# Adding the products of four pairs of states ahead of W_out, with other ranks and tiles, in a four-layer kernel

## The chip, the cores and the metric

The kernel runs on one core of a Trainium2 chip. Time is device time of one execution in microseconds. TensorE is called PE here (its weight loads PEld), VectorE DVE, ScalarE ACT, GpSimd POOL, and SyncE, which issues most DMAs, SP.

## The reference

The input is 16 sequences of 256 tokens of width 128, all float32. Four residual layers follow each other, each on a layer norm of x:

- attention whose softmax weights are summed to one over the keys and multiplied with the query's own v, so that it amounts to a linear map: `x + norm(x) @ W_v @ W_out + b`;
- a mixture of 8 experts with hidden width 512, of which each token takes its best two by gate logits, weighted by a softmax over the two: `sum_e w_e * relu(x @ w1[e]) @ w2[e]`;
- a selective state space with 16 states: `delta = softplus(...)`, for each state n a scan over the 256 positions of a sequence, and

```
xs = cumsum(dB_u * dA_cumsum, axis=1) / (dA_cumsum + 1e-12)
y = einsum('bldn,bln->bld', xs, C) + u * D
out = y @ W_out + b_out
```

- a second mixture of experts with the same weights and the same kind of gate.

## The kernel before

The 4096 tokens are cut into eight blocks of 512 (two sequences). In the first experts' layer the blocks are taken in the groups `FIRST = ([0], [1], [2, 3], [4, 5], [6, 7])`, in the second in `SECOND = ([0, 1], [2, 3], [4, 5], [6], [7])`. `attention` and `gate` prepare blocks, `route` ranks the tokens of each expert and scatters their rows to a DRAM buffer `slots` (POOL's indirect DMAs), `experts` works through a group's eight experts, `collect` gathers two rows for each token (POOL again) and adds them to x, `mixer` is the state space of one block, and `finish` stores a block.

`SLOTS` gives the room for each expert in a group of one, two, three or four blocks, for each of the two layers. A room over 512 or 128 rows is divided evenly: 192 becomes two tiles of 96 rows, 330 three of 110, 216 two of 108, 384 three of 128. In `experts` an SP DMA fetches a tile `xs` from `slots`; PE transposes it; four matmuls with w1 (`ps_b<-xsT,w_s`), relu `h`, four matmuls with w2 that add up in one bank (`ps_y<-h,w_s`), a copy `yT`, transposes back, a copy `yr`, and an SP DMA to `ys`, from which `collect` gathers (`yy<-ys`). A group's gathers wait for its last `ys`. If an expert has more tokens than its room, a general path runs behind the kernel.

In `mixer` the 16 states are worked off in eight pairs. For a pair, ACT makes two decays and two `th` (tanh); PE spreads the rows of B and C over the partitions (`ps_B`, `ps_C`, two bf16 matmuls each); DVE multiplies `ps_B` by `du`, scans it with the decay into `w`, makes `ps_C = (th + 1) * ps_C` and `th = ps_C * w`. `th` has four buffers, `w` three, the decay two, `ps_B` and `ps_C` one each. Ahead of the pairs a block makes `delta`, `z`, `lt` and `du`, and one matmul with W_out's scaled copy `wsd_s` starts `ps_s`.

The products `th` of two pairs are added up (`ADD = 2`), and then two matmuls with `wsh_s` add the two halves to `ps_s`:

```
group.append(th)
if len(group) > 1:
    product(group[0], group[0], th, ALU.add)
if len(group) == ADD:
    for k in range(2):
        matmul(so, wsh_s, group[0][:, k, :], False, n + k == NS - 1)
    group = []
```

Nothing is issued where it is written. Each operation is recorded as a job of a class `Plan`, with the engines that may do it. `product` may go to POOL or DVE, `copy` and `relu` to ACT or DVE, and normalizing to ACT or DVE. `ORDER` is a long string of packed ranks, one for each job; `Plan.order()` places the jobs in time by these ranks, with a duration for each from `cost()` (DVE, ACT, POOL) and from `matmul`, and so settles both the order on each engine and which engine does a job. The program is then issued in that order. So the ranks and the durations matter to the program only through this order and these choices. For that reason all jobs have the same line in the profile, L710, but for the scatters (L807), the gathers (L821) and a few others. The functions that the change touches and their callers:

Of the kernel before, what the change touches and what calls it, by code (L numbers as in the profile page):

```python
# [10 lines left out]
F32 = mybir.dt.float32  # L11
# [3 lines left out]
AF = mybir.ActivationFunctionType  # L15
ALU = mybir.AluOpType
# [12 lines left out]
SECOND = ([0, 1], [2, 3], [4, 5], [6], [7])  # L29


SLOTS = ((192, 330, 480, 632), (216, 384, 600, 800))
UNIT = 2
ADD = 2
JOIN = 2
ACC = 0
POOLED = (3,)
# [3 lines left out]
XN, ROW, XS, XT, H, YT, DEPTH = 4, 3, 4, 3, 4, 3, 3  # L41

ORDER = (
    "c-oy;3zS?{m92a3_kHWtzxw}AcS6!hI-~;z$O;57;6V8Q2_u0S5d^_uSc)<WMU9}iM3yW-9GO9x!6gH;R9KFnMgszpL;?f?f"
    "k*<R^Xq@t@4Y*x(n)u9Rdv$gbywAU_uY5jJ?HGR&pu3!7%XbbZAPKv1@3dL7-PWr9y>~ce89&%(C@K%Jo9!(hVu?i`7ck&TU"
    "=}!eF%Vl)_8eOGlzoV+GCP40*uyj))&`!j{^V`L0}L96gZ<4gs;O)2b>A*3(6>rA1qHftKE)g1PD&+d4C53zj>tYtuRmST4)"
    "&WZ=i;-Wdt8&k}Jkz4frZfW0dx>2F9<qDP7bBq>YMzaZlQu8;l;?+ePSH#x<oKoEc04YdQ9_z#2UcR8YkQZ@_JKUIwrXpCBw"
    "y%n$|z+H*Fet87`^C*_nH1fcC_oYqiEa5-i%s&Llw`v@46X#t7>ItB=v6B`tD>z8D<E*H}0f-#>loAIJY14hsV+|<5QxV>F6"
    ">MACb|KehA*xQaiirRK`r;~{cLjneDt0Nf|kEoo*U@p9_j!i#dWsezvrR+sxshv)zuWsGhFh-7pml~U+|6RMg#e{BnBi1OJ8"
    "{AtKz1A~GTIhQXQRn%ke_1+;3-()<bWZJRR6xkpvtH^UoJyCT1TFBd-vKZw{l=N5^8I7n;k;oMd;@Ct0ds)?$Q&UmPXz}F6#"  # L50
    "dW9?-*SWOvxor10@uUMTT|4)h($^?t#9+p%<8@UwC4u_H&;{uTgXsAMiMbl@4dSA0RXZ4ACKM^vhG!qIZ3nF^_^|>`d-Tn&K"
    "wyzk<LlLQRB1Sh~zY_bopU;AF}%AS(s#+{Wm8iwK;{49U2`nGz1AY|+UEUrmJ%G;LyF9NZ`WH88wyQ>luGWVmKT3OV<!#{EW"
    "z!NIr5>A!W@A}UR$AWI|yFk+BEncN=R!(&QNPwlz&?wY>(L5$Xj@WkfMZ5@g#l8cWfdX#yell3CZhJqETdv4Sl?uKS~-)v})"
    "*4Vd22ckBKk|8VVy=0BLVS=}uE1S@ZYfgCSgm>u8<lgqPqc<;kc?rNJurWMKMhvbR2qEm+|2UcJKs<96Vvpuj0d3D4Ol{~jD"
    "cbd9cbIWM858=Cz7YhCRBII%{;(YO>*0hKYgrutqLc+%P%RBi3%*?jzD0>I3<3Efd@<bwI+I<3KauaD-H2gE37^e)@TEs7Rl"
    "mCTe(M@e{Hq2=o>!CxJnq#en9mpN*lS+&Iw2j!+`ts4{f2PVMHH#yYYq^BZsi=|-|t8(JfC6;{iqKJpA{YQK>8{db}Y7%1%m"
    "$WPD1#pR5Rju3=MF*JyEdPx|=W?&I655)808;G9f7ezWWA3XfwvOg@aHMUvd&5l5TnkS>p^$u;L$4aYP5jbo}#ADG_H0DKuj"
    "u!Z7tjkurLfov96nM^nzTX@8{Q$937vRW0C-5uOb^Oj3%l#B4<#!j~c5E#e_fwC;J+RCpwK|NPft1JPleU~<FVRNIdf6eaz_"
    "Nv0P>Z+A!CEICH}&6*u~1??PyUf7eg8@uY%b;<r%k|>f-k1T$sZg1Me)YxXVdWNeW?%8tuHdp{3#ogBbYA;w0bivzZvubm=S"
    ";u|tWYNdXxF6B#=HHK)3%~O5?RK;+SsOX+qgTI%sagY#bZ33c{lh?fXeo(UeK9XlQ!l>}&R7jB33OpT{afUf*+^D_6L!6*c<"  # L60
    "h7L9m@!!-^s_fy|QfmDvDt?3h}Vp{*$OLDcCS%nsc8svmPfsu)&;TDFcKF;EU}a@<8*34~xXDg|A}%sHpKTeo9dE`>kiXNE!"
    "2}Rao~0CdHr>Vh5vv;!0oyH0!d8k45OvgXmyL7+J<Yl^FG(U|O>XL3Z^p+mWlK0Gj2vl>bFE98-Xh<|d<ttXm_ycw_46$d*="
    "N{H*TW<G$1MvHzy|X*oCAKl|_DUET4E2{EZ~6~SV(+hdkJ2eiw&E}+CZo)u}D7<-j8X)h}#*5`2TRY(d%ak`I(om3YX7XQ;-"
    "82r-(aOFxjFT(DFH3&d<{WUmyg<*(gK;*T8E51PH6`c5O%$++arQY0k=N}_YL3^ZMXC|Hk8Tkp7kug{EMoc)KVA>SNEd*jOR"
    "9YC!pixRCZz|TuC8>TjE2Sd2j>|k}_jex`*77FX%xVN5;iP64HL+aT94Q(>1jRGe9_6W#Uzmtbw}b7x^s&|tS_9HVKCt5A<r"
    ";K3#2~{Q$LJJ~Hs`_xjttq@*ZSwWyjf2SC@AZj@tRoMK)SD!2#kI>vgzGf`??{<_J?ayD>|GN-@g6sACYC`O>cGby6Yag{&{"
    "i}+$XP#SP|(-qF~Kw%fXLgv}ls@Vcf(y{7%z2MX{bU?!9o?c~7re&u%04nm5av&iTz*iXBTg#+qYc$6S5>Z_diGZg@Lf6Z@l"
    ")wW4G;Y_;oS5sUq}{^J@BankP?#tvB!n0-i|(&S41wf@8QeqzI@v|6^xKn>E_@SbQwN(5yWll87$l4ZQ+dV~^R$DnXlPzYRo"
    ")nh#23O4sr7AdIyNKVav-OU8V&iXsz8B^JL-v%twpAwQ=Qp|pL-T}0+fY4v3M`J_Ct2}NOAeM^U#$*H;)v^arT5v56Py~LZy"
    "KtG#Z#A8=wV{w6{Aq2UK4;F$;&&I4XD{lhb2fGEE&R*a#-{EVssn+QktixhOrgXABzgXo6auRe$x$=KXq4BsUH~Xp{8b1kln"  # L70
    "N+6lChLhmik8mt@M}Y;tMZR#K=n$X_u5IpFss8+P{mW+v!LiI0f_TD5d!MEHHWJ{fMhI2>AeM8WT~lFC&MDJMTtfyM<#FVQG"
    "6lvYlzEg5Xy?ijwILJC0%|7jEaAdM4HQ9Ul^>ZtxO2d*7_vQ`_~SaB^+CfzpN?51RLemBMwz*BO@dmSRRDbMiV)Q)90R8v)z"
    "PHZ9pW?~U#))Iqb7HGfO(OYbK0V2jtFoI3HtT9vb*jfliR`xD_|=fpUst#pJqUfuD|?7`1i9dy4PmcQ6C_ua2TI`NL#X@*mg"
    "FRefEuh)`e$Qz<7@yzC)%_k#wz7<VN(?nT?jN!h38#$$@B&A}fNhKD)_V3C>6?W_Km;UG4d2i226s4(^Prc~oj9DzqGETcK8"
    "l1I%Z`po^mmqr`!`l4Z+3U}RBpKnhl}a~$D~2#N!gR!o$meVKHLX;2^h2XY87cFhMkAv)*fxxquK9mk7i_+QICRJ`ksSbxqM"
    "*I8qi^KK9B8|S>`kad*b*wWhc}`O7B-;)d)e~yQKVGI!z@(HG(2T0$>Pb^WShXEOR;`2lv#Y9kQb>_Ogj2i=fq_yU67CeVZr"
    "{@gsGEVbJj_oU$d>DPTCh!;?-g}h~-P|d6M0v5E0K_4$xYQ1gxnot`W$KR~PH@`L`l|7UC;<sTQxWUQ6||poTy22!i!IhKzy"
    "pXQf3l-Gg!A-@Dv~rsY^rO)gVE@UZZmD)VdP0}msHuac5QY{JGYJL#qvpHEjmiedOSa1F&HY|ulVc)O@cHts`I{@eiBjwR(!"
    "_8ix^k!l0(h~&T7vM4e5KVN*DYOK3E+dhbWdb3?O^7)&A1eAW?=7Vz!2K8hi*_g1DL}BPd81oY)3j%rzwa6$#het4-Ihzya7"
    "77H$j6raj9Caxc6jsy)rla2BZ#kLR!ussM?-TivyE_K=-%6eQ%Dy}IKPmF8KGQE(BPY{&sD0aUkypJowK$5&pz3Zxld!;r4b"  # L80
    "i{@8#QJ_IFn*;{VzcdLVpURg@j=$V-dy;p8g9$&<0E*5r}RnW4ssP!0vkwhv!q5M?mqtJQ-&7z$ANdJr>3`CNU5J!(3K065A"
    "i+L-$}&JeEnTAef=kA}-sw&-e>J#HChX&52<yMomPBiDcydpfxkF<esn+mybj<nYg@AEfou;>8oatI$$gl&*zUTVA&_w=>d0"
    ")VuxalN-e>{1?hHd#T<gEY603Sq;ya#Gqh_Mm3NVtcv12paWEAp@N;jl_QKli;?LCjg<s`!{TB$IU6ISyA=LpWVI7x57}ZFu"
    "UyR@ii5A&vj>Y+kR=nMcOp1blceu7K&ZmLJKbnmXE#R8F_*sih9<z#X+;A%6{A{Ez$^$XzqzsgPamGSd;v$zQUxv|TBU}pJO"
    "amc?{~0On8j*%t>`(S5uz_(gF0ig2eO`~@C)l`YfsL7i$mXvUPy{QQMzyN>t{N*$*BV(<B)RH{Zi?qJ-47zZD6A6QTNl6PX5"
    "ISpC}NRp5Pnd{WL_F(JZ&*EA26kJwh%tbQBz`jL{MqK*a1OmW2Y&=;)dCIpY+M<9hn6WW0SGk%=for-_rsND|HXUrYeDY^Wt"
    "uRc9iXm1sqF%8mqwdiz%BgB3yFq0D1xK{)d$SD=|z!!`R#$kn*RmVr&^uNvVT^94rO$#9JszL!=M5ANyV03eex*#vqAJ5%Ny"
    "4jqAju=(&N=4uCL$VU#40LZNbPG?#1NILG;DwkqZqSz2uCi;rN@$1`Lu><|JJbQm8p-oY1<G0KV!2gME%*-8+W+2sVI7iO}V"
    "by#4#`*ZG+D5_>`9E(B_QH4OGPsRbTmB)28Dj{m%J|AhKbS}aVhfpCwQ3T%8MPLEt0_hZ!m=-&iwY`GPJ764^K~`KA)|>;ZT"
    "@}ro$BSFRTs>(OgIUG3@gF-FYys&tR|0K7L5=Q1R;Acpqk2X^1mlt)<4r;#9V#Ar;xBaY8bA8LwH`k|bnD=W9={Cqp~?6mho"  # L90
    "&4_Wy<Nnt3%6`4o`d?Jc7`~W)6IU(A0xWeYE66moHm&C{%Swf1)8>zM4L0V)e(guDC4q`lQj5u0A+aaZ8un3Qd1Ymv1sxdPR"
    "bXpF`2ny4=hvZmZ(jB1TFvQ!y*3d@871G&uZwjyQCLcvtak_0a06QK|H{u2@M=iF$eXLNf~A_>t8mIX5}CBwCXxTAHI}2I<h"
    "`E~}xkx}PS^I0)w{z$;7M(mMgE@bH1*P=z1LhC|cMJ}fL|GOVkadMHZ|Iwe#A`toNgp%6N%#M5OoJ7Xx|oBi^Al<r1{j)cBY"
    "l~?L1sL<2Fxe}N<G+K_!DGWB1<tAJ`9fwY^rJe?ox=L6Hjs_FgT9+F+bp=uascEUaWHugt_1Qsn0t`Y``6H-EgwhO|E(3LFi"
    "Z?4fSLUZ9QdC9!r$s_l{2aE7_!YHqVmIU{%F`z!%!=I%kKZ5%&Cmzc%b~}~q>IM!rb81tqy!K!VUCYqq#7$!!==bhCX=3s;$"
    "%^*;wCa3OO-O9o(ZQ-hqNQio)L;mia^O(WxDCmOmSION~THP!{KuJTjQtx^z2P$M2bgM$Pd4pP-rZqEAXmI7_yZA^bv5zLiv"
    "(<9@0~Uc6m5-C3WfQIGd(iPb1aJH#rlw)TN|RU9cU3796-NOrQ-8{Em$WuY$d&)W2z2U6(ZvewlXCrKM0GRTY^=ugp-!=%Y&"
    "Fsu8My`l0<!hGyKW_?@eYMLo3~SMyobTC68?dK%$h)m{3q^-@n)MyH}zA67bsj(WIKz)be3x{NFe<qcAG^{A`%9Fy8f&&*3R"
    "YdmMxAO$n(YeN$ybbOaV6%8^2zS1*j2oGzV{zTp1(Yv#Z&O`qXwp16!"
)  # L100


# [491 lines left out]
def tile_layers(  # L594
# [117 lines left out]
    def cost(engine, name, views):  # L712
        n = max(v.free_size() for v in views)
        if engine == "DVE":
            t = 0.15 + 0.00208 * n if "scan" in name and n > NE else max(0.2, 0.15 + 0.00104 * n)
            return t + 0.08 * sum(v.free_size() == 1 for v in views[1:] if n > 1)
        if engine == "ACT":
            t = 0.16 + 0.00085 * views[0].free_size()
            return t + 0.1 * sum(v.free_size() == 1 for v in views[1:] if n > 1)
        if name == "tensor_tensor":  # L720
            return max(1.4, 0.2 + 0.0021 * n)
        return 0.1 + 0.001 * n
# [57 lines left out]

    def matmul(out, lhsT, rhs, start=True, stop=True, **order):
        n = rhs.free_size()
        took = max(0.25 if n <= 16 else 0.42, 0.00178 * n) if rhs.dtype == F32 else max(0.06, 0.00044 * n)
        k = dict(out=out, lhsT=lhsT, rhs=rhs, start=start, stop=stop)
        return plan.job(
            [("PE", took, call(nc.tensor.matmul, (), k))], [out], [lhsT, rhs], **order
        )
# [501 lines left out]
    def mixer(b, r, m):  # L1289
# [58 lines left out]
        for n in range(0, NS, 2):  # L1348
# [36 lines left out]
            group.append(th)  # L1385
            if len(group) > 1:
                product(group[0], group[0], th, ALU.add)
            if len(group) == ADD:
                for k in range(2):
                    matmul(so, wsh_s, group[0][:, k, :], False, n + k == NS - 1)  # L1390
                group = []
# [115 lines left out]
```

## Time and profile before

| what | before |
| --- | --- |
| median of 14 runs | 724.43 us (720.0 to 734.24) |
| the profiled execution's own time | 728.65 us |
| its span | 726.9 us |
| mean granted clock of PE | 0.915 |
| busy: PE, DVE, ACT, POOL | 627.2, 555.2, 487.8, 416.5 us |
| first product of a mixer | 127.6 us |
| end of the last scan | 626.7 us |
| last matmul into `ps_s` ends | 632.9 us |
| last `ys` issued | 703.4 us |

The busy times are sums over the span; an engine's idle time has a releaser in the profile, the event that ended it. A group of instructions is written with its output, its inputs, their shapes, how often it occurs, and then its busy time and the mean duration of one. A float32 matmul has two records in the trace, so the 64 matmuls with `wsh_s` stand there as 128.

### The profile page before, as it was taken

What the parts mean: (1) busy time and instruction counts of PE and PEld (TensorE: products, weight loads), DVE (VectorE), ACT (ScalarE), POOL (GpSimd) and SP (SyncE); (2) the same over time, 40 slices, a digit from 0 to 9 for tenths busy, and PEclk for the clock granted to TensorE, in tenths of its full rate; (3) what the DMA queues carried; (4) which work ended last, traced back from release to release, by engine and by line L of the source; (5) the groups of instructions that cost most, each with busy time, mean ns of one, the idle gap of its engine ahead of it and who ended that gap; (6) DMA issues with size and microseconds to landing.
All of it is one profiled execution on the core that took longest, in us unless ns stands there. A gap on an engine that the chain in (4) does not pass through costs nothing. (4 is left out here: it accounts for less than half of the span.)

```text
span 726.9 us, 8786 instructions
## 1 busy us (share of the span) xinstructions
PE 627.2 (86%) x2598; PEld 391.9 (54%) x2598; DVE 555.2 (76%) x1038; ACT 487.8 (67%) x996; POOL 416.5 (57%) x490
## 2 busy tenths in 40 slices
PE   5488999799999769899898889787999999999971
PEld 4366877465645226565344555333555455578860
DVE  4765448999988798899999898998989988740120
ACT  2243538988967797679989677788877764455440
POOL 5367771497075458677944852864137886314743
PEclk9557999999999889799999999889999999999995
DMA  8931331211330001421123210120112521213342
GB/s 228 334 113 52 94 99 42 81 45 48 87 86 19 1 30 46 118 63 34 31 68 83 56 33 26 54 60 23 49 44 71 154 61 56 82 46 102 100 136 76
DMA packets 76373, 55.05 MB, mean 76 GB/s; under 512 B 8064, under 2 KB 69152, under 8 KB 76320
## 3 DMA queue, kind: packets, MB, share of 16 engines
q1 hardware_dynamic: 66464, 37.35, 17.7%
q0 software_dynamic: 8192, 16.79, 8.1%
q10 hardware_dynamic: 1664, 0.29, 0.2%
q8 instruction: 22, 0.36, 0.2%
q14 instruction: 31, 0.25, 0.1%
HBM read 27.09 MB, written 27.32 MB: 75 GB/s over the span
## 5 line engine op out<-in xcount | busy, mean ns | idle before, releaser
L710 PE MATMUL ps_b<-xsT,w_s 128*128 128x330 f32 (+3 forms) x640 | 211.7, 439 | 16.3 <-ACT h L710 7.1
L710 PE MATMUL ps_y<-h,w_s 128*128 128x330 f32 (+3 forms) x640 | 213.3, 423 | 3.3 <-ACT yT L710 2.1
L821 POOL DMA_INDIRECT yy<-ys,of x128 | 126.8, 990 | 100.9 <-DMA ys<-yr 38.4
L807 POOL DMA_INDIRECT slots<-row,to x128 | 126.5, 988 | 80.3 <-issue 22.1
L710 ACT ACTIVATE h<-ps_b 128x384 f32<-128x384 f32 (+2 forms) x234 | 110.1, 476 | 89.3 <-PE ps_b L710 87.0
L710 PEld LDWEIGHTS ps_b<-xsT,w_s 128*128 128x128 f32 x640 | 115.3, 197 | 75.0 <-ACT h L710 24.6
L710 DVE TENSOR_TENSOR_SCAN w<-decay,ps_B 128x1024 f32<-128x1024 f32 x64 | 145.8, 2279 | 0.2
L710 PEld LDWEIGHTS ps_y<-h,w_s 128*128 128x128 f32 x640 | 109.6, 194 | 45.1 <-issue 12.0
L710 ACT ACTIVATE th<-later,lneps,ha_s 128x512 f32<-128x512 f32 x128 | 100.2, 809 | 6.5 <-DVE th L710 2.9
L710 ACT ACTIVATE decay<-delta,nea 128x510 f32<-128x510 f32 x128 | 86.7, 714 | 4.2 <-DVE w L710 3.1
L710 DVE TENSOR_TENSOR ps_B<-du,ps_B 128x1024 f32<-128x1024 f32 x64 | 78.2, 1222 | 13.6 <-PE ps_B L710 13.0
L710 DVE SCALAR_TENSOR_TENSOR ps_C<-th,ps_C 128x1024 f32<-128x1024 f32 x56 | 68.3, 1219 | 7.5 <-PE ps_C L710 7.3
L710 PE MATMUL ps_s<-th,wsh_s 128*128 128x512 f32 x128 | 70.5, 643 | 3.9 <-POOL th L710 3.8
L710 DVE TENSOR_TENSOR th<-ps_C,w 128x1024 f32<-128x1024 f32 x56 | 67.9, 1213 | 0.2
L710 POOL TENSOR_TENSOR th<-th,th 128x1024 f32<-128x1024 f32 x20 | 47.2, 2359 | 29.4 <-DVE th L710 27.0
L710 POOL TENSOR_TENSOR rstd<-var,root 128x8 f32<-128x8 f32 (+1 forms) x20 | 28.2, 1412 | 52.7 <-DVE var L710 49.9
L710 PEld LDWEIGHTS <-sel 96*128 96x128 bf16 x256 | 25.7, 102 | 58.3 <-issue 47.4
L710 PE MATMUL ps_B<-pieces,sel 96*128 96x512 bf16 x128 | 41.5, 397 | 10.1 <-DVE w L710 10.0
L710 PE MATMUL ps_b<-ident,yT 128*110 128x128 f32 (+3 forms) x208 | 43.6, 279 | 2.9 <-ACT h L710 1.5
L710 PE MATMUL ps_b<-ident,xs 110*128 110x110 f32 (+3 forms) x208 | 38.8, 277 | 7.3 <-ACT h L710 3.2
L710 PE MATMUL ps_C<-pieces,sel 96*128 96x512 bf16 x128 | 41.2, 401 | 3.3 <-DVE th L710 3.2
L710 PEld LDWEIGHTS ps_b<-ident,xs 110*128 110x128 f32 (+3 forms) x208 | 26.6, 148 | 26.3 <-ACT h L710 8.6
(161 smaller groups left out, 815.4 us busy)
## 6 DMA issues: line engine op xcount, KB each, us to landing
slots<-blank SPq DMA_DIRECT2D x3, 1536.0 KB
xs<-slots SPq DMA_DIRECT2D x24, 192.0 KB
ys<-yr SPq DMA_DIRECT2D x24, 192.0 KB
w_s<-in_w SPq DMA_DIRECT2D x16, 256.0 KB
xs<-slots SPq DMA_DIRECT2D x24, 165.0 KB
ys<-yr SPq DMA_DIRECT2D x24, 165.0 KB
xT<-in_xT SPq DMA_DIRECT2D x8, 256.0 KB
slots<-row,to POOLq DMA_INDIRECT x128, 2.3
```

Of the source, the lines that this page charges most:

```text
L710: return lambda: f(*[real(x) for x in a], **{n: real(x) for n, x in k.items()})
L807: inst = nc.gpsimd.indirect_dma_start(out=real(out), out_offset=bass.IndirectOffsetOnAxis(ap=real(rows), axis=0), in_=real(in_), in_offset ...
L821: nc.gpsimd.indirect_dma_start(out=real(out), out_offset=None, in_=real(in_), in_offset=bass.IndirectOffsetOnAxis(ap=real(rows), axis=0), ...
```

## The change

`ADD` becomes 4, so that the products of four pairs are added up before two matmuls take them into `ps_s`: six adds and four matmuls for a block instead of four adds and eight matmuls. A new first branch, for `ADD == NS // 2`, is not taken (4 is not 8). `SLOTS` gives 336 for 330 (tiles of 112 rows for 110) and 208 for 216 (104 for 108). The durations by which the jobs are placed are changed, and the ranks are new ones.

```diff
-SLOTS = ((192, 330, 480, 632), (216, 384, 600, 800))
+SLOTS = ((192, 336, 480, 632), (208, 384, 600, 800))
 UNIT = 2
-ADD = 2
+ADD = 4
...
 ORDER = (
...
         if engine == "DVE":
-            t = 0.15 + 0.00208 * n if "scan" in name and n > NE else max(0.2, 0.15 + 0.00104 * n)
-            return t + 0.08 * sum(v.free_size() == 1 for v in views[1:] if n > 1)
+            out, *ins = views
+            ins = [v for v in ins if v.free_size() > 1]
+            fast = name in ("tensor_scalar", "tensor_copy") and not any(
+                v.home.psum or v.dtype != F32 for v in (out, *ins)
+            )
+            t = 0.15 + (0.00208 if "scan" in name and n > NE else 0.00052 if fast else 0.00104) * n
+            return t + 0.07 * sum(v.free_size() == 1 for v in views[1:] if n > 1)
...
         n = rhs.free_size()
-        took = max(0.25 if n <= 16 else 0.42, 0.00178 * n) if rhs.dtype == F32 else max(0.06, 0.00044 * n)
+        took = max(0.23 if n > 16 else 0.2, 0.0017 * n) if rhs.dtype == F32 else max(0.06, 0.00044 * n)
...
             if len(group) > 1:
                 product(group[0], group[0], th, ALU.add)
-            if len(group) == ADD:
+            if len(group) == ADD == NS // 2:
+                product(group[0][:, 0, :], group[0][:, 0, :], group[0][:, 1, :], ALU.add)
+                matmul(so, wsh_s, group[0][:, 0, :], False, True)
+            elif len(group) == ADD:
                 for k in range(2):
                     matmul(so, wsh_s, group[0][:, k, :], False, n + k == NS - 1)
                 group = []
```

## The prediction

> **What bounds the kernel now.** I read the page's busy line and its forty slices first, then the engines' busy time by stage, the costliest groups, the waits of the mixers' stage, and single instructions on TensorE.
>
> ```profile
> PE 627.2 (86%) x2598; PEld 391.9 (54%) x2598; DVE 555.2 (76%) x1038; ACT 487.8 (67%) x996; POOL 416.5 (57%) x490
> PE   5488999799999769899898889787999999999971
> DVE  4765448999988798899999898998989988740120
> PEclk9557999999999889799999999889999999999995
> ```
>
> No engine is full throughout, so the average decides nothing. I cut the span at the first product of a mixer (127.6 us) and at the end of the last scan (626.7):
>
> ```profile
> 0.00:127.60 127.60, 99.94 (x521) 82.08 (x521) 74.89 (x353) 55.58 (x141) 70.56 (x130) 0.83 0.47 137
> 127.60:626.70 499.10, 448.39 (x1664) 246.81 (x1663) 456.88 (x616) 390.98 (x761) 306.02 (x312) 0.94 0.20 57
> 626.70:726.90 100.20, 78.85 (x417) 63.03 (x415) 23.45 (x71) 41.27 (x96) 39.91 (x48) 0.89 0.31 90
> ```
>
> The columns after the length are PE, PEld, DVE, ACT and POOL busy, then the granted clock. In the 499.1 us of the mixers DVE works 456.9 and PE 448.4: two engines nearly full, each idle some 42 to 51 us because the other is late. In the last 100 us PE is nearly alone. In the first stage PE is full only at its end.
>
> ```profile
> L710 DVE TENSOR_TENSOR_SCAN w<-decay,ps_B 128x1024 f32<-128x1024 f32 x64 | 145.8, 2279 | 0.2
> L710 DVE TENSOR_TENSOR ps_B<-du,ps_B 128x1024 f32<-128x1024 f32 x64 | 78.2, 1222 | 13.6 <-PE ps_B L710 13.0
> L710 DVE SCALAR_TENSOR_TENSOR ps_C<-th,ps_C 128x1024 f32<-128x1024 f32 x56 | 68.3, 1219 | 7.5 <-PE ps_C L710 7.3
> L710 DVE TENSOR_TENSOR th<-ps_C,w 128x1024 f32<-128x1024 f32 x56 | 67.9, 1213 | 0.2
> L710 PE MATMUL ps_s<-th,wsh_s 128*128 128x512 f32 x128 | 70.5, 643 | 3.9 <-POOL th L710 3.8
> L710 POOL TENSOR_TENSOR th<-th,th 128x1024 f32<-128x1024 f32 x20 | 47.2, 2359 | 29.4 <-DVE th L710 27.0
> ```
>
> Four DVE instructions of a pair of states take 2.28 + 1.22 + 1.22 + 1.21 = 5.93 us, on 64 pairs 360 to 380 us of the stage. DVE waits on PE in that stage for these:
>
> ```profile
> DVE ps_B L710 <- PE ps_B L710: 13.0, 14, 2.4
> DVE ps_C L710 <- PE ps_C L710: 7.3, 11, 1.8
> DVE h L710 <- PE ps_b L710: 6.2, 5, 3.1
> DVE yT L710 <- PE ps_y L710: 4.0, 3, 2.7
> ```
>
> That is 30.5 us of the 42. ps_B has one buffer: the matmuls of the next pair wait for the scan of this one, and the next product waits for them. So the two engines are coupled pair by pair, and whatever PE has queued between two pairs counts against what DVE has.
>
> **The change part by part.** Counts are those of the two programs' instruction orders; a DVE duration is reduced by 0.063 us, since the 1038 rows sum to 620.9 us against 555.2 busy (each overlaps the next).
>
> *Matmuls into W_out.* Eight per block become four: 32 fewer. Back to back one costs what lies between its start and that of what follows:
>
> ```profile
> 620.34 1.02 PE L710 MATMUL ps_s<-th,wsh_s 128*128 128x512 f32 x2
> 621.20 0.60 PE L710 MATMUL ps_B<-pieces,sel 96*128 96x512 bf16 x2
> ```
>
> 0.86 us at full clock, 27 us in all, nearly all in the mixers' stage.
>
> *Adds.* Four per block become six: 16 more. The orders put 4 of them on DVE (12 to 16) and 12 on POOL (20 to 32). DVE: 4 x 1.16 = +4.6 us, not hidden. POOL: 12 x 2.36 = +28 us, where POOL has 193 us free in that stage; as it also loses 8 products of 1.27 us, +18 net. Each group's matmuls wait for its last add, and everything behind them in PE's queue with them; PE and PEld waited 3.8 + 5.9 us so before, and there are half as many groups: -5 to +5, I take nothing. The first th of a group is held over four pairs instead of two, out of four buffers; ACT needs 3.05 us a pair (two decays, two tanh) against 5.93 on DVE and waited 2.9 us on it in all, so nothing, at most 3.
>
> *POOL against DVE.* While POOL added x and yy at 424 us, a DVE comparison with two SBUF inputs took 3.2 us instead of 0.2; in the mixers' stage I count 7 us of such stretching. With 18 us more of POOL work in 306: +1, bounds 0 and +4. It is taken into the range only.
>
> *Work moved between DVE and POOL or ACT.* In the mixers' stage the products of delta, z and du come to DVE 9 times more (+5.7), relu of 330/336 columns 7 more and of 384 three fewer (+1.5), copies of xnT 4 more (+2.5), normalizing and row scaling (+1.9), th from ps_C one (+1.2), against 2 fewer of delta from PSUM (-1.3), 3 fewer x + yy (-1.9) and small ones (-1.9). With the adds, DVE's sum in the stage goes from 454.7 to 467.0: **+12.3 us**.
>
> *Tiles.* The 192 matmuls of up and of down at 330 columns, two records for one: 192 x 0.010 = +1.9 us; those at 216 columns, 128 x 0.014 = -1.8 us. Nothing on PE. The issue of ys on SP takes
>
> ```profile
> L710 SPq DMA_DIRECT2D ys<-yr x12: 551/573/638, 79.1 to 124.0; - x12
> L710 SPq DMA_DIRECT2D ys<-yr x19: 550/821/843, 130.9 to 296.0; - x19
> ```
>
> 0.57 us for 96 rows and 0.82 for 110. From a group's last issue to its first gather go 3.0 us with 96 rows and 3.9 with 110, so at the most 0.9 us for each of three groups, hidden, since PE has other work then (waits of PE on xs: 0.7 us in the run). The last group of all, 108 rows, is issued at 703.44 and gathered from
>
> ```profile
> 708.25 0.94 POOL L821 DMA_INDIRECT yy<-ys,of  x1 [4.21 <-DVE x L710]
> ```
>
> 104 rows I put at the same 4.8 us (bounds 3.0 and 5.5). [...]
>
> *Sum by stage, PE at full clock.* Before the first mixer product: PE 68.7 to 74.1 us, because the gate of a third pair of blocks and a few more expert matmuls now come before it. PE is busy 32.3 of the last 33.6 us there, but only 67.6 of the 94 before; so between 0 and +7 (5.4 us at the granted 0.83 are 6.5), and I take **+3**, the middle.
>
> Mixers' stage: PE 400.9 to 377.6, DVE 454.7 to 467.0. If DVE's 42 us of idle time stay, +12. If PE's relief takes 20 of the 30.5 us of waits, -8. Pair by pair: the sum over the 63 intervals of the larger of DVE's and PE's work (PE at clock 0.94), DVE cut at the product or at the scan, gives 491.6 or 504.3 before, with the measured 499.1 between them, and 518.6 or 524.1 after: +20 to +27. The new order places PE's expert work less evenly against DVE: the largest mismatch after is a pair in block 7 with 21.6 us of PE beside 9.1 of DVE. Over four pairs at a time the same sum grows by 10 only. I take **+12**, nearest the row that is not in doubt (DVE's own work), between -8 and +27.
>
> End: after the last matmul into ps_s PE has about 61.5 us of expert work instead of 70, but block 7's gate, scatters and fetch (632.9 to 666.7, 34 us) and its own experts bound it to 64. **-6**, between -8.5 and -3. From the last expert output to the end 23.9 us stay: issue, eight gathers of 1.25, add, transposes, output.
>
> +3 + 12 - 6 = +9 on the profiled execution, whose time is 728.65 (span 726.9 and 1.75 around it): 737.6. The 14 runs have a median of 724.43, 0.9942 of that: **733 us**.
>
> **A rule against it.** By stretches of 40 us, PE was slower where it had least to do: 29.4 us busy from 240 to 280 with clock 0.79, against 39.75 busy and clock 1.00 from 520 to 560. So part of the 27 us is lost again: at 0.94 to 0.90 the remaining 378 us cost 18 more. That is inside +27. [...]
>
> **The rivals.**
>
> *PE is the bound and its relief counts.* For it: 30.5 us of DVE's waits are on PE, and 23 us of PE work leave the stage. Against it: DVE's own sum grows, and the pairs fit worse. It decides once these waits fall by more than 11 us (the +9 above and the 2 that can be measured). With a fall of 20: first stage 0, mixers 12 - 20 = -8, end -6, so -14: 710 us.
>
> *The sums cancel.* The mixers' stage +3, first stage +3, end -6: 724 us. Decided by DVE's waits on PE falling by 9 of 30.5.
>
> *The order is the bound.* The pairs' mismatch shows in full, +20 to +27, with +3 and -3 for the stages around it: 744 to 751 us. It has the sign of my forecast and the pair sum for its price.
>
> *The change does not do what it says.* If an expert had more tokens than a tile's room, the general path would run. The reference routes at most 176 tokens to one expert where the room is now 208, and 310 where it is 336. Excluded.
>
> **How the numbers follow.** Forecast (+5 to +16 on the profile's scale) 0.37; the order as the bound 0.21; cancelled 0.11; PE the bound 0.31. Slower takes the first and the second, less a little. About 0.3% (2.2 us) is what a measurement can tell here. So faster 0.31, same 0.11, slower 0.58. The range leaves out a tenth on each side: the better half of PE's case down to 711, and of the order's case up to 748.
>
> **What would show it.** Right: ps_s records fall from 128 to 64, POOL's th<-th,th rises to 32, DVE's busy time in the mixers' stage rises by about 12 us, the waits of DVE on ps_B and ps_C stay near 20 us, the last scan ends about 15 us later, and from there to the end it takes 6 us less. Wrong: the waits on ps_B and ps_C fall below 8 us and the stage is shorter than 495 us (PE was the bound); or they rise above 35 us (the order); or POOL's adds are waited for by ps_s with more than 10 us.

## The result, and the profile after

The changed kernel takes 767.01 us (median of 10 runs, 762.23 to 769.06) against 724.80 us for the kernel before in the same comparison: a ratio of 1.0569, with a 95% interval of 1.0546 to 1.0593 (it is the ratio of the means, without two runs of the kernel before that took over 1.5% longer than its fastest; that of the medians is 1.058). It is 42 us slower. The forecast was 733 us with a range up to 748, so the sign was right and the size was not.

The profiled execution has a span of 765.8 us and a mean granted clock of 0.876 (before 0.915). Its page begins with the busy line and the forty slices:

```profile
PE 619.8 (81%) x2534; PEld 389.9 (51%) x2534; DVE 577.9 (75%) x1067; ACT 484.1 (63%) x979; POOL 438.7 (57%) x498
PE   4467999799879886996689998739699599999880
DVE  3864555799999989999999999898899968942110
PEclk9656989899989989997699999569799889999995
```

PE's row now has holes late in the mixers (3, 6 and 5, where the clock row has 6, 7 and 8); DVE's row is as full as before. I cut the span at the same two marks as before, the first product of a mixer (now 140.2 us) and the end of the last scan (668.7). The columns after the length are busy time of PE, PEld, DVE, ACT and POOL, then the granted clock:

```profile
0.00:140.20 140.20, 106.64 (x567) 90.93 (x567) 80.38 (x377) 56.87 (x150) 80.13 (x145) 0.81 0.44 130
140.20:668.70 528.50, 442.69 (x1582) 239.80 (x1582) 476.41 (x623) 389.93 (x743) 318.38 (x306) 0.89 0.19 54
668.70:765.80 97.10, 70.43 (x387) 59.19 (x385) 21.07 (x70) 37.27 (x88) 40.19 (x49) 0.88 0.30 85
```

The first stage grew by 12.6 us, the mixers' stage by 29.4, and the end shrank by 3.1: 38.9 us together, the difference of the two spans. The last scan ends 42 us later, where the prediction had 15. In the mixers' stage DVE is busy 19.5 us longer and idle 9.9 us longer. PE lost 23 us of matmul work at full clock and is busy only 5.7 us less, since its clock there went from 0.94 to 0.89.

The waits of DVE on PE in that stage, and then those of PE on DVE (total us, times, longest):

```profile
DVE ps_B L710 <- PE ps_B L710: 23.7, 22, 2.6
DVE h L710 <- PE ps_b L710: 5.6, 6, 2.5
DVE ps_C L710 <- PE ps_C L710: 3.5, 7, 0.7
```

```profile
PE ps_C L710 <- DVE th L710: 18.8, 16, 3.0
PE ps_B L710 <- DVE w L710: 17.3, 9, 3.6
```

Before, those two waits of PE were 3.2 and 10.0 us. So both engines wait more for each other: DVE for the pair's matmuls, PE for the pair's buffers. With one buffer each for `ps_B` and `ps_C`, neither can run ahead; that each wait hands the other engine a later start follows from this, and no row shows it by itself. The groups that the change names:

```profile
L710 PE MATMUL ps_s<-th,wsh_s 128*128 128x512 f32 x64 | 37.4, 673 | 3.9 <-DVE th L710 3.8
L710 POOL TENSOR_TENSOR th<-th,th 128x1024 f32<-128x1024 f32 x32 | 75.4, 2356 | 54.9 <-DVE th L710 45.8 <-ACT decay L710 5.1 <-ACT h L710 3.3
```

The records of `ps_s` are halved and POOL's adds went from 20 to 32, as announced, and the matmuls wait once, 3.8 us, and not for POOL.

### The profile page after: what moved, and what is told of

Its sections match the earlier page's. It is cut to its first block, busy times and chain, and to the rows that moved or that the text cites. A ratio compares the mean times of both kernels' runs of the same rounds, so it can differ in the third digit from the quotient of the medians.

```text
span 765.8 us, 8667 instructions
## 1 busy us (share of the span) xinstructions
PE 619.8 (81%) x2534; PEld 389.9 (51%) x2534; DVE 577.9 (75%) x1067; ACT 484.1 (63%) x979; POOL 438.7 (57%) x498
## 5 line engine op out<-in xcount | busy, mean ns | idle before, releaser
L710 PE MATMUL ps_b<-xsT,w_s 128*128 128x336 f32 (+3 forms) x640 | 219.5, 456 | 18.4 <-DVE r L710 6.5
L710 PE MATMUL ps_y<-h,w_s 128*128 128x336 f32 (+3 forms) x640 | 213.0, 429 | 2.9 <-ACT yT L710 2.8
L812 POOL DMA_INDIRECT slots<-row,to x128 | 130.3, 1018 | 63.6 <-issue 24.5
L710 PEld LDWEIGHTS ps_b<-xsT,w_s 128*128 128x128 f32 x640 | 119.8, 205 | 77.3 <-ACT h L710 21.8
L710 PEld LDWEIGHTS ps_y<-h,w_s 128*128 128x128 f32 x640 | 112.2, 196 | 45.5 <-issue 12.0
L710 POOL TENSOR_TENSOR th<-th,th 128x1024 f32<-128x1024 f32 x32 | 75.4, 2356 | 54.9 <-DVE th L710 45.8
L710 DVE TENSOR_TENSOR th<-ps_C,w 128x1024 f32<-128x1024 f32 x56 | 67.9, 1213 | 0.2
L710 PE MATMUL ps_b<-ident,xs 112*128 112x112 f32 (+3 forms) x208 | 40.3, 292 | 17.0 <-DMA xs<-slots 4.5
L710 PE MATMUL ps_b<-ident,yT 128*112 128x128 f32 (+3 forms) x208 | 44.2, 289 | 10.3 <-ACT xsT L710 3.9
L710 PEld LDWEIGHTS ps_b<-ident,xs 112*128 112x128 f32 (+3 forms) x208 | 28.2, 156 | 36.2 <-issue 6.8
L710 ACT COPY yr<-ps_b 128x384 f32<-128x384 f32 (+3 forms) x69 | 30.2, 440 | 19.0 <-PE ps_b L710 18.5
```

Of the source, the lines that this page charges most:

```text
L710: return lambda: f(*[real(x) for x in a], **{n: real(x) for n, x in k.items()})
L812: inst = nc.gpsimd.indirect_dma_start(out=real(out), out_offset=bass.IndirectOffsetOnAxis(ap=real(rows), axis=0), in_=real(in_), in_offset ...
```

## The experiments

Most kernels below have their order written out: instead of placing jobs by ranks and durations, the program is issued in the order (and with the choice of engine for each job) that one of the two kernels has, but for the named edit. So a part of the change can be made without a new order, and a new order without the part. What is put in stands in an order that was planned without it. Where an edit concerns only the order or the engines, its diff is given in words, and longer code is shortened. The first four and the last two ran on chips on which the kernel before takes 798 us, the others where it takes 724 to 727 us; ratios are always against the kernel before on the same chip.

### The parts of the change, each alone

**e1, four pairs and the new tiles in the order before.** The 16 new adds stand directly behind their products.

```diff
-SLOTS = ((192, 330, 480, 632), (216, 384, 600, 800))
+SLOTS = ((192, 336, 480, 632), (208, 384, 600, 800))
-ADD = 2
+ADD = 4
```

> The instructions of the kernel before in their old order on every engine (the order written out, no placing anew), with ADD = 4 and the new tiles; the sixteen new adds stand right behind the product of their pair, five on DVE and eleven on POOL, and the matmuls of the first half-groups are gone. If the new order alone is responsible (theory), the time is within 8 us of the kernel before: 27 us of PE work less, 6 us of DVE more, so 717 to 731 us. If the adds and matmuls or the tiles are responsible (rival), it is slower by most of the 42 us: 750 to 767.

Measured: 817.57 us, ratio 1.0251 [1.0174, 1.0328]: some 20 us slower where the theory allowed at most 7, so four pairs cost time in the order before too.

**e2, four pairs alone in the order before.**

```diff
-ADD = 2
+ADD = 4
```

> As the run before it, with the old tiles: the adds and matmuls alone. Theory of the order: 717 to 731 us. Rival (the adds): 750 us or more. Difference to the run with the new tiles too: the tiles, at most 2 us.

Measured: 816.50 us, ratio 1.0257 [1.0164, 1.0350]. A wait of ACT appears, since a group's first `th` keeps its buffer over four pairs:

```profile
ACT th L776 <- POOL th L776: 22.9, 10, 6.0
```

**e3, the new tiles alone in the order before.** The first two lines of e1's diff.

> The kernel before in its own order with tiles of 112 and 104 rows alone. Theory of the order: within 2 us of 724.5, at best 3 us less, since three groups' rows can be gathered some 0.9 us sooner each. Rival (the tiles): over 735.

Measured: 796.36 us, ratio 1.0007 [0.9960, 1.0054]. The tiles cost and bring nothing that can be measured (the interval is some 4 us wide to either side).

**e4, the new order with four pairs and tiles undone.** The order of the changed kernel, with `ADD = 2` and the tiles before.

```diff
-SLOTS = ((192, 336, 480, 632), (208, 384, 600, 800))
+SLOTS = ((192, 330, 480, 632), (216, 384, 600, 800))
-ADD = 4
+ADD = 2
```

> The changed kernel's order on every engine with ADD = 2 and the old tiles: sixteen adds fewer, 32 matmuls into ps_s more, each pair of them right behind its add. Theory of the order: still slow, 760 to 780 us (the matmuls cost up to 27 us of PE, where PE is late; the adds give back 4 on DVE). Rival (adds, matmuls and tiles responsible): 725 to 740.

Measured: 875.30 us, ratio 1.0957 [1.0870, 1.1044]. The loss is not in `ADD` alone: with two pairs, as before, the new order is slower still.

**e9, the new order with two pairs and the new tiles**, on a chip where the kernel before takes 726.7.

```diff
-ADD = 4
+ADD = 2
```

> The changed kernel's order with ADD = 2 (16 adds fewer, 32 matmuls more, each pair of them right behind its add), new tiles kept. Theory (two separate losses, the adds on a full DVE, some 9 to 13 us, and the new order, some 30): 755 us or a little less if only DVE counts, up to 775 where PE is short of time in the new order's crowded pairs. Rival (the adds are at the root of it, and the order merely follows): 725 to 740.

Measured: 800.74 us, ratio 1.1044 [1.0972, 1.1116]. That is 33 us over the changed kernel (767.58 us in e5, on another chip with nearly the same time for the kernel before), for 27 us of PE work put back and 16 adds taken out: here the PE work put into the new order shows in full and more.

**e8, four pairs in the order before, with a fifth buffer for th.**

```diff
-        u = new("u", [P, TB], bufs=3)
+        u = new("u", [P, TB], bufs=2)
-        d = new("delta", [P, TB], bufs=3)
+        d = new("delta", [P, TB], bufs=2)
-            th = new("th", [P, 2, TB], bufs=4)
+            th = new("th", [P, 2, TB], bufs=5)
```

> The kernel before in its old order with ADD = 4, as in the run of the adds alone, but five buffers of th in place of four (two of u and delta in place of three pay for it; the old order never holds more than two of these). Theory of the held buffer (ADD = 4 lost in the old order because ACT's tanh waits for POOL's add to set a th free, 23 us of such waits, and the relu behind it in ACT's queue waits too): those waits fall under 5 us and the ratio to the kernel before goes from 1.026 to 1.00 or below. Rival (the adds on DVE and POOL themselves): it stays above 1.015.

Measured: 737.02 us, ratio 1.0175 [1.0102, 1.0248]. ACT's wait is down to 8.2 us, not below 5, the ratio is far above 1.00, and the stage is 8.7 us longer than before:

```profile
127.80:635.60 507.80, 434.90 (x1602) 236.87 (x1601) 468.73 (x621) 389.77 (x760) 330.55 (x318) 0.93 0.20 56
ACT th L776 <- POOL th L776: 8.2, 4, 3.7
```

DVE's busy time rose by 11.9 us. Its five new adds make 5.8 of that; the rest is that other DVE instructions became longer. I count this as excess: for each instruction of the stage that took more than 1.2 times the median of its form, the time above that median. It was 7.6 us before and is 14.0 here, with 11 more adds on POOL.

**e11, the relief of PE alone:** e8 with the 16 new adds left out, so that a part of the sum is missing; PE has half the matmuls into `ps_s`, and nobody has more to do.

```diff
-            if len(group) > 1:
+            if len(group) > 1 and n // 2 % 4 != 2:
```

> The old order with ADD = 4 and five buffers of th, but without the sixteen new adds: the products of the third and seventh pair of states are left out of the sum. So PE's relief of 32 matmuls (27 us) stands alone. Theory (DVE sets the pace): only 2 to 8 us faster than the kernel before. Rival (PE sets the pace): 15 to 20 us faster.

Measured: 719.37 us, ratio 0.9914 [0.9884, 0.9944]. 27 us of PE's work taken away bring 6 us:

```profile
127.60:620.70 493.10, 429.93 (x1602) 236.73 (x1601) 454.64 (x616) 389.98 (x760) 304.01 (x312) 0.93 0.20 58
```

DVE is busy 454.6 of these 493.1 us, 2 us less than before, and its idle time fell by 3.8 us (42.2 to 38.5).

**e13, the same in the new order:** the changed kernel without the 16 new adds.

> The changed kernel without the sixteen new adds (products of the third and seventh pair of states left out of the sum): the same work as the old order's run with the relief alone, which took 0.991 of the kernel before. So the ratio of the two is the order alone. Theory (the order loses 30 us whatever the adds): 750 to 760 us, ratio to the kernel before 1.035 to 1.05. Rival (in the new order, too, most is the adds'): 725 to 740.

Measured: 766.47 us, ratio 1.0537 [1.0436, 1.0638].

```profile
138.40:665.60 527.20, 446.36 (x1582) 240.96 (x1582) 467.48 (x618) 389.78 (x743) 291.18 (x297) 0.89 0.19 54
```

e11 and e13 have the same matmuls and adds (the tiles differ, which cost nothing, and the fifth buffer, where ACT waits 0.8 us in e13) and differ in the order and its choice of engines. The quotient of their ratios is 1.063, within 0.011 either way. Of the 41.9 us between their spans, 10.8 lie ahead of the first product, and the end gives 3.0 back. In the stage the new order makes DVE 12.8 us busier, since its choice of engines gives DVE more to do, and 21.3 us idler. The same two waits of e11, and then of e13:

```profile
DVE ps_B L776 <- PE ps_B L776: 16.9, 16, 3.2
PE ps_C L776 <- DVE th L776: 5.8, 10, 1.1
```

```profile
DVE ps_B L775 <- PE ps_B L775: 27.5, 23, 2.6
PE ps_C L775 <- DVE th L775: 18.8, 15, 3.0
```

This is the main result: the new order, with its choice of engines, costs about 6% at equal work. Half of that is idle time of DVE in the mixers' stage, and half of this idle time, 10.6 us, is the wait on `ps_B`; PE's wait for DVE at `ps_C` grows by 13.0 us beside it.

**e10, the old kernel with its adds on POOL.** The order before; its 12 adds on DVE go to POOL.

```diff
-DVE: 12 of 32 adds th<-th,th
+POOL: the same 12 adds, at the same place in the order
```

> The kernel before, its order untouched, with its twelve adds on DVE moved to POOL in place: 14 us less on DVE, 28 more on POOL. Theory (DVE sets the pace of the mixers' stage, and POOL's adds cost DVE about 0.4 us each by holding up instructions with two SBUF operands): 3 to 9 us faster than the kernel before. Rival (PE sets the pace): within 2 us, or slower where matmuls into ps_s wait for the longer adds on POOL.

Measured: 738.71 us, ratio 1.0149 [1.0090, 1.0208]. DVE's own work fell by 12 adds, and its busy time did not fall:

```profile
127.80:635.40 507.60, 450.50 (x1662) 245.97 (x1661) 455.76 (x605) 391.11 (x759) 328.64 (x318) 0.94 0.20 56
```

455.8 us for 605 instructions, against 456.9 for 616 before. The excess rose from 7.6 to 18.3 us. Two groups of DVE, before and in e10:

```profile
L710 DVE TENSOR_TENSOR oh<-lg,top 128x64 f32<-128x64 f32 x6 | 4.3, 713 | 0.0
L710 DVE TENSOR_SCALAR lt<-z 128x512 f32<-128x512 f32 x8 | 3.4, 423 | 0.0
```

```profile
L777 DVE TENSOR_TENSOR oh<-lg,top 128x64 f32<-128x64 f32 x6 | 6.5, 1078 | 0.0
L777 DVE TENSOR_SCALAR lt<-z 128x512 f32<-128x512 f32 x8 | 6.2, 770 | 0.0
```

The means hide that single instructions were held up. The longest `oh<-lg,top`, before and in e10, and the POOL adds beside it (start, duration):

```profile
424.38 3.20 DVE L710 TENSOR_TENSOR oh<-lg,top 128x64 f32<-128x64 f32 x1
425.14 2.35 POOL L710 TENSOR_TENSOR th<-th,th 128x1024 f32<-128x1024 f32 x1
```

```profile
427.86 5.39 DVE L777 TENSOR_TENSOR oh<-lg,top 128x64 f32<-128x64 f32 x1
428.50 4.66 POOL L777 TENSOR_TENSOR th<-th,th 128x1024 f32<-128x1024 f32 x2
```

The median of this form is 0.22 us. Both times it ended 0.09 us after POOL's last add.

### What could be wrong with the new order

**e5, the changed kernel again**, as the base of this group.

> The changed kernel, every engine's order written out and nothing else touched: the yardstick for the other runs on this chip. Every theory: the ratio to the kernel before stays near 1.057.

Measured: 767.58 us, ratio 1.0582 [1.0486, 1.0677].

**e6, five early copies back on DVE.** In the changed kernel ACT issues 12 DMAs and loads a table before its first copy; the new order put five early copies there.

```diff
-ACT: wtmp<-bv_s, wtmp<-bo_s, batt, wat, one first copy of x
+DVE: the same five
```

> The changed kernel with five early copies (the spread bv and bo, batt, the merged weights wat, one x) on DVE in place of ACT, whose queue is busy with twelve DMA issues and a table load until 10.5 us. Theory (part of the first stage's 12.6 us is lost at these copies): 3 to 5 us faster than the changed kernel, all of it ahead of the first mixer product. Rival (the first stage is late through the third pair's gate alone): within 1 us of the changed kernel.

Measured: 763.74 us, ratio 1.0513 [1.0415, 1.0612]. The reason for the edit is seen in the timeline of the changed kernel (start, duration), and against it that of the kernel before:

```profile
9.19 1.28 ACT L710 ACT_TABLE_LOAD   x1 [9.19 <-DMA bdt_s<-in_b_dt]
10.48 0.30 ACT L710 COPY wtmp<-bv_s 128x128 f32<-128x128 f32 x1
```

```profile
4.37 0.23 DVE L710 COPY wtmp<-bv_s 128x128 f32<-128x128 f32 x1 [4.37 <-DMA bv_s<-in_bv]
```

The first attention output came 3.2 us earlier than in e5 (19.46 for 22.68 us), but the first product of a mixer only 0.9 us earlier (137.4 for 138.3), less than the 1.9 us by which the two profiles of the changed kernel differ there (140.2, and 138.3 in e5). So these copies are part of the late start, and that they count at its end is not shown.

**e12, the gate of a later pair of blocks moved back.** 71 instructions that the new order has ahead of the first mixer product go behind it.

```diff
-gate of the third pair of blocks, ahead of the first ps_B
+the same 71 instructions, behind the first product of the first mixer
```

> The changed kernel with the 71 instructions (34 on PE: the gate of blocks 4 and 5 and some of the second group's experts) that the new order does ahead of the first mixer product, and the old one behind it, moved back to the same pair of states that they follow in the old order. Theory (the first stage's loss comes from this work): the first mixer product 5 to 8 us sooner, the whole 3 to 8 us faster than the changed kernel. Rival (they only fill gaps of PE there): the first product at most 2 us sooner, the whole within 3 us or slower.

Measured: 797.48 us, ratio 1.1011 [1.0928, 1.1093]. The first product came at 139.5 us instead of 140.2, although PE had 101.8 us busy before it instead of 106.6; and the mixers' stage took 558.0 us. The amount of PE's work ahead of the first product does not set its time.

**e7, PE kept busy.** 112 matmuls with zeros into `ps_s`, two ahead of the `ps_B` of each pair but a block's first, against the low clock.

```diff
+            for _ in range(2 if n else 0):
+                matmul(so, none, pieces, False, False)  # none is zero, bf16
```

> The changed kernel with two bf16 matmuls of zero weights into ps_s ahead of every pair's matmuls into ps_B but a block's first (112 in all, 24 us of PE at full clock), which PE can do while it waits for DVE. Theory of the clock (in the mixers' stage the granted clock fell from 0.94 to 0.89 because PE has less to do, and that eats its relief): the stage's clock rises to 0.92 or more and the time falls by 3 to 12 us, though PE works more. Rival (order alone; the clock is a by-product): the time rises by 0 to 15 us.

Measured: 782.17 us, ratio 1.0796 [1.0719, 1.0873]. The clock of the stage rose from 0.89 to 0.90 only, and the stage took 543.6 us. So the run does not support that the low clock costs the time, but it hardly raised the clock and cannot exclude it. For the first stage there is an answer: it took 140.2 us at a clock of 0.81 in the changed kernel, and 141.5 us at 0.98 in e16 below, which has the same order but for 18 products given to another engine:

```profile
0.00:141.50 141.50, 108.02 (x567) 91.79 (x567) 80.04 (x372) 56.28 (x150) 82.51 (x143) 0.98 0.43 128
```

**e16, 18 products from DVE to POOL** in the changed kernel, against the products that the new order had moved to DVE.

```diff
-DVE: 18 products (delta, z, du, x + batt, x + yy), 14 of them in the mixers' stage
+POOL: the same 18
```

> The changed kernel with the eighteen products (delta, z, x + batt, x + yy) that went from POOL to DVE given back to POOL in place: DVE 11 us less, POOL 23 more. Theory of the prediction (DVE's own added work is 12 us of the loss): 5 to 11 us faster than the changed kernel. Rival (a product on POOL holds up DVE nearly as long as it takes on DVE, and takes longer itself): within 3 us or slower.

Measured: 766.88 us, ratio 1.0548 [1.0482, 1.0615]. DVE's busy time in the stage fell by 6.3 us to 470.1, its idle time rose by 5.7; the stage took 527.9 us instead of 528.5.

### How much either engine's work is worth

**e14, half of the matmuls with w2 left out, order before;** **e15, the same in the changed kernel.** The experts' output is then the half of its sum.

```diff
-                for c in range(NFC):
+                for c in range(0, NFC, 2):
```

> The kernel before with two of the four matmuls of the second expert product (half of the hidden width is left out): 160 float32 matmuls less, some 74 us of PE in the mixers' stage alone. Sum over the pairs of the larger of DVE's and PE's busy time in its trace: 479 to 463. Theory (DVE sets the pace in the old order, but for PE's crowded pairs): the mixers' stage 15 to 25 us shorter, of 74 taken from PE; the whole 25 to 40 us. Rival (PE sets the pace): 50 us or more in that stage.

> The same half left out of the changed kernel. The sum over pairs goes from 499 to 482. Theory (loss through DVE's own time and a PE that stands idle where the new order has no expert work for it): the mixers' stage falls as in the old order (15 to 30 us) and stays 20 us or more longer than the old order's. Rival (loss through PE's crowded pairs alone): it falls by 35 to 45 us and comes within 10 us of the old order's.

Measured: e14 716.95 us, ratio 0.9868 [0.9795, 0.9941]; e15 750.84 us, ratio 1.0316 [1.0247, 1.0385]. The mixers' stage of e14 and of e15:

```profile
126.30:619.00 492.70, 413.40 (x1478) 217.04 (x1479) 460.50 (x616) 389.18 (x760) 304.02 (x312) 0.92 0.20 58
```

```profile
137.10:658.80 521.70, 409.68 (x1398) 208.46 (x1399) 477.15 (x623) 386.97 (x744) 318.80 (x306) 0.87 0.19 55
```

In e14 PE is busy 35 us less in the stage, and the stage is 6.4 us shorter; in e15 33 us less, and 6.8. Both are less than half of the 15 us that were expected at the least. The new order still has 521.7 us with PE busy 410, so PE's amount of work is not its bound.

**e17, the old kernel without its adds on DVE.** Its 12 adds on DVE are replaced by 24 more matmuls; **e18,** all 32 adds by 64 matmuls. The edit holds for those adds alone.

```diff
-                product(group[0], group[0], th, ALU.add)
+                for k in range(2):
+                    matmul(so, wsh_s, group[0][:, k, :], False, False)
+                group[0] = th
```

> The kernel before in its order, with the twelve adds that stand on DVE left away and the two halves taken into ps_s by matmuls of their own (24 more, each pair of them behind the matmuls into ps_C of the next pair of states, where its product is done): 14 us less on DVE, 21 more on PE. Theory (DVE and its waits pace the stage; PE's work counts about a fifth of its length): 6 to 12 us faster. Rival (PE paces): 10 us slower or more.

> The same for all 32 adds: none left on DVE or POOL, 64 matmuls more (55 us of PE at full clock, where PE stands idle for some 51 us of the stage). Theory: DVE loses 14 us of adds and some 5 of being held up by POOL, PE's idle time is used up: between 10 us faster and 10 us slower than the kernel before. Rival (PE paces): 40 us slower.

Measured: e17 816.04 us, ratio 1.0232 [1.0177, 1.0287]; e18 852.81 us, ratio 1.0699 [1.0638, 1.0760]. 24 matmuls of 0.86 us are 20.6 us of PE, and the kernel lost 18.6; 64 are 55.0 us, and it lost 55.3. Both went as their rival had it. DVE's saving brought nothing: from e3 (another chip, on which the kernel before takes as long) to e17 its busy time in the stage fell from 460.7 to 443.5 us and its idle time rose from 72.5 to 104.5:

```profile
141.70:674.90 533.20, 463.25 (x1662) 253.13 (x1662) 460.70 (x616) 392.12 (x760) 303.63 (x312) 0.91 0.19 54
140.60:688.60 548.00, 479.49 (x1704) 257.43 (x1703) 443.51 (x605) 390.33 (x759) 302.04 (x312) 0.93 0.18 52
```

On these chips DVE is idle 72.5 us before anything is added, against 42.2 where the kernel takes 725 us, so added PE work need not show as fully there.

## Why the prediction was wrong

On the profiled execution the forecast was short by 29.9 us (767.5 for 737.6): 9.6 in the first stage, 17.4 in the mixers', 2.9 at the end. In the mixers' stage 7.2 of them are DVE's busy time (+19.5 for +12.3) and 9.9 its idle time, which was put at no change.

**The tiles** were put at nothing, and e3 shows it. The row behind it was the issue of `ys`, 0.82 us for 110 rows and 0.57 for 96; the tiles of 112 rows now read

```profile
L710 SPq DMA_DIRECT2D ys<-yr x16: 550/556/576, 170.2 to 294.8; - x16
```

so 0.56 us for 112 rows; the issues of 104 rows took 0.84 us (median of 16), those of 108 rows before 0.78. What sets these durations no run shows, and no time follows from them.

**The matmuls into W_out and the adds** were counted rightly (64 records, 32 adds on POOL). DVE's own work was put at +12.3 us, and measured were +19.5. Of the rest 4.7 us are the *hold-up of DVE by POOL*, the term that was left out of the sum and put into the range at 0 to 4: the excess rose from 7.6 to 12.3 us. 2.5 us are small rows that I did not trace. The term was sized by the wrong rule: 7 us of stretching for the whole of POOL's 306 us, so much per us of POOL's work. What matters is which DVE instruction meets a POOL operation. In e8 the excess grew by 6.4 us for 11 more adds on POOL and in e10 by 10.6 for 12, but in e14 by 5.1 (to 12.7) with POOL's operations unchanged. In the changed kernel 2.0 us of it stand beside POOL's adds (3.0 before) and 10.1 beside its other products (4.3 before); without the 16 new adds (e13) it is 9.3 in all. So neither the new adds nor the new order alone is its source.

**"PE is the bound and its relief counts"** fell. It needed DVE's waits on PE to fall by 11 us. e11 gives the relief alone its price: 6 us for 27, less than a quarter, since DVE's idle time fell by 3.8 us only. With the adds it turns into a loss of 13 us (e8).

**The mixers' stage, +12,** is the step that failed, and by most: it measured +29.4. Three numbers lay on the table, -8, +12 and +20 to +27, and I chose the middle one on the ground that it rested on the row that was not in doubt, DVE's own work. That takes DVE's 42 us of idle time as a constant that the new order keeps. It is not: it measured 52.1 us, and e13 against e11 shows 21.3 us more of it from the order alone. The pair sum, which weighs PE's and DVE's work between each two products, had the sign and nearly the size. Taken from the busy times of the traces, the larger of the two engines' work, product to product, sums to 474.8 us before and 494.1 after (scan to scan 478.6 and 496.4). So the misfit of the pairs holds 18 to 19 of the 29.4 us; the other 9 to 10 are time inside the pairs in which the fuller engine is idle as well, and no sum of work contains them. That the planned sum came as near as 27 is in part luck. The pair in block 7 that it named as the worst, 21.6 us of PE beside 9.1 of DVE, took 22.8, with PE busy 22.4 and DVE 14.3:

```profile
613.30:636.10 22.80, 22.43 (x74) 12.64 (x75) 14.33 (x28) 12.63 (x24) 13.58 (x13) 0.92 0.25 70
```

So the rival "the order is the bound", given 0.21, was the one that came nearest, with the pair sum a little short (27 for 29.4) and its total, 744 to 751, further short, because of the first stage. Its mark in the text, waits on `ps_B` and `ps_C` above 35 us, was not met: they were 27.2. The waiting went both ways, and I had named only DVE's half.

**The first stage, +3,** failed too, beyond its bound of +7: it measured +12.6. I had priced PE's work before the first product; e12 shows that this is not what sets it. The delay grows along the chain of routing: the first attention output comes 4.3 us later, of which 3.2 are the five copies that ACT does late (e6), the eighth `ys` 7.4 later (100.7 for 93.3), the first gather 9.3 (105.7 for 96.4), the second addition of gathered rows 11.3 (119.5 for 108.2), the first product 12.6. At the gather it is POOL's queue:

```profile
103.87 1.67 POOL L710 TENSOR_TENSOR rstd<-var,root 128x8 f32<-128x8 f32 x1 [4.61 <-DVE var L710]
105.73 1.03 POOL L826 DMA_INDIRECT yy<-ys,of  x1 [0.19 <-DMA xs<-slots]
```

The `rstd` of another block now stands ahead of the gathers and waits 4.61 us for DVE; from the eighth `ys` to the gather go 5.0 us, and 3.1 before. This is an instruction moved past another in one queue, which the change's order showed and I did not price. As e6 took back 3.2 us at the start and won 0.9 at the product, the delays do not simply add, and I did not try each of the others.

**The end, -6,** measured -3.1, within its bounds of -8.5 to -3: from the last `ps_s` to the last `ys` 69.7 us (674.3 to 744.0) against 70.4 (633.1, by the end of the last record, to 703.4), so almost all of the expected shortening of PE's expert work did not come, and why is open; 1.7 us came after the last `ys`: that 104 rows would take the 4.8 us of 108 from the issue to the gather was an estimate that no run shows, and the gather followed after 3.4 us.

**The rule against it** was put inside +27. Here the row speaks more clearly than before. In the timeline of the changed kernel the clock falls from 1.00 to 0.50 after short waits only (start, duration, in brackets the idle time before):

```profile
476.00 0.59 PE L710 MATMUL ps_C<-pieces,sel 96*128 96x512 bf16 x2 [0.52 <-DVE th L710]
477.83 1.11 PE L710 MATMUL ps_b<-ident,xnT 128*128 128x128 f32 x4 [1.24 <-ACT yr L710]
...
484.09 1.06 PE L710 MATMUL ps_C<-pieces,sel 96*128 96x512 bf16 x2
```

From 470 to 477 us the clock is 1.00, from 478 to 495 it is 0.50; the single waits of PE from 455 to 478 are at most 1.32 us, and PE was busy 1.2 of the 3 us from 474 to 477, just before the fall. The two matmuls of `ps_C` take 1.06 us instead of 0.59. What makes the clock fall no run shows. Whether the clock's loss is a cause in the mixers' stage or a companion is open, since e7 hardly changed it.

**What is open.** Why this order makes the two engines wait for each other so often is shown only down to the pairs, and its choice of engines was not parted from its sequence but for the 18 products of e16. It is not cured by less PE work (e15), less DVE work (e13, e16), a busier PE (e7), or the gate put back (e12). Which of its moves is to blame was not found. The costs also do not add up: four pairs alone cost 1.75%, the order alone about 6%, the two together 5.7%, because in the new order the 16 new adds cost nothing that can be measured (e13 1.0537, the changed kernel 1.0569). No version with the whole computation beat the kernel before.

## What to carry to other kernels

Where two engines are coupled step by step through a single buffer and both are about 90% full, work out the sum over the steps of the larger engine's work, and do not let it stand as a mere end of the range: here it was nearer than either engine's total, in this one case. PE work put into a finished order showed in full (18.6 of 20.6 us, 55.3 of 55.0, 33 of 27), and work taken out of one showed in part only (6 of 27 us and 6.4 of 35 of PE's, 0.6 of 6.3 of DVE's). So a change that takes 27 us from one engine and gives 5 to the other can lose. A re-planned order is a change of its own: follow each instruction that stands anew ahead of a critical one in its queue, from the first stage on.

## What the runs showed of the hardware that was not expected

A DVE instruction that stands beside a tensor operation of POOL can be held up until that operation is over, as `oh<-lg,top` was in e10 (5.39 us instead of 0.22). It happens to few: in the mixers' stage before, 7.3 of the 7.6 us of excess lie in six instructions that overlap a tensor operation of POOL, and none of these six has a `ps_` tile among its operands. The four long instructions of a pair, all with a `ps_` tile, overlapped such operations 85 times and gained 0.2 us together. So there is no fixed price of an add on POOL (2.36 us). On the average the added ones cost DVE 0.6 us each in e8 and 0.9 us in e10, where twelve adds moved from DVE (1.16 us net each) left DVE's busy time in the stage at 455.8 us instead of 456.9. `oh<-lg,top` has two inputs in SBUF; `lt<-z`, with one such input, was held up as well, once for 3.19 us in e10 instead of 0.42. What DVE and POOL share there no run shows. In the kernel before, the 512 elements of `lt<-z` take 0.83 ns each (423 ns), where the 1024 of `th<-ps_C,w` take 1.18 (1213 ns).
